# Words of eight marks instead of four in the scan of a sparse graph stack, built on TensorE and read by VectorE out of PSUM

## The chip, the cores and the metric

The kernel runs on one core of a Trainium2 chip. The metric is the device time of one execution in microseconds (us). The engines are called as the profile calls them: PE (matrix multiply; PEld loads its weights), DVE (vector), ACT (activation), POOL (which here mostly issues gathers, that is, DMAs whose rows are given by an index list), and SP (which issues the other DMAs). The program gives each engine its instructions in one fixed order.

## The reference

Four graph layers follow each other on x of 4096 rows by 128 features, with one adjacency matrix adj of 4096 x 4096 in f32, of which only few entries differ from zero (all of the diagonal does, and row 0 is the densest; the chance of an entry falls with both indices).

```python
h = relu(layernorm(x)); x = x + (h @ Ws.T + (adj @ h) @ Wn.T + b)                         # layer 0
h = relu(layernorm(x)); x = x + (h @ w0 + (adj @ h) @ w1 + (2 adj @ (adj @ h) - h) @ w2 + b)  # layer 1
h = relu(layernorm(x)); H = h @ W.T                                                        # layer 2
tau = adj.T * exp(leaky(alpha_src + alpha_dst));  x = x + (adj.T * tau / tau.sum(1)) @ H
h = relu(layernorm(x))                                                                     # layer 3
agg[i] = sum_j adj[i, j] * gelu(s[i] + d[j] + b);  x = x + layernorm(gelu([h, agg] @ U.T + b) + h) * w + b
```

Layer 3 takes each single non-zero entry (i, j) with its value. So the kernel has to find where the entries are.

## The kernel before, in words

All work is done for the entries that are likely to be there, and a dense version follows only if something was missed. The rows stand in an order fixed beforehand, in which each of the 32 blocks of 128 rows has about as many entries as fit whole chunks of 128.

**Scan.** `read_adj` (L761) loads each block's 128 x 4096 values in two halves of 1 MB on SP, into three buffers. `mark` (L770) turns a half into marks on ACT: one byte of fp8 an entry, 1.0 where the value is positive and 0.5 where it is zero. There are four mask tiles of 128 x 4096 bytes. `scan` (L781) takes a block's mask on DVE: it takes the mark off the diagonal (L787, after which `bare[b]` is set), and reads four marks at a time as one 32-bit word. L791 takes the largest word of each stripe of 256 columns into `col_raw`; L796 puts the word's own number (from the constant `spread`, 0 to 1023) into the bits that all marks share; L798 sets words without an entry to zero; and MAX8 (L805) takes the eight largest words of each segment of columns into `cand`. The segments were cut so that a row hardly ever has more than eight words with entries in one. After L798 and after the row flags the mask tile is given back (`mask_left`).

**Row and column lists.** A row stripe is 256 rows (two blocks), a column stripe 256 columns. `row_flags` (L693) finds with matmuls of the mask against a column of ones (L704) which blocks' columns have entries; `col_flags` (L713) takes the same for columns from `col_raw`, once `all_marked` is set, that is after L791 of the last block. Both then take one of three **lanes** (sets of small tiles, `lane = yield lanes`), set their flags (L709, L717), and run `pairs` (L635), a chain over DVE, PE, ACT and DVE that ends in lists of rows to fetch (`fetch_row`, `seg_row`; `fetch_col`, `seg_col`). The lane is then given back. `pairs` uses one of three `bank` and two `pick` banks of PSUM.

**Layers.** For layer 0 POOL gathers, for each chunk of a row stripe's list, 128 segments of adj.T (`rseg`) and 128 rows of h (`g`); the blocks next to the diagonal and the dense ones are loaded whole (`big`). PE sums both (L1146, L1163). `finish_0` adds the result, makes the next h and writes it to a table in memory, from which layer 1 gathers its rows once the whole table is there. The segments are kept in `r_tab` for layers 1 and 2. `fetch_columns` (L739) gathers column segments (`cseg`) for layer 2's attention.

**Entries.** `entries` (L813), for eleven groups of units (a unit is a row block, or a part of block 0), counts the marks of the candidate words on DVE, ranks them, spreads the words over partitions with matmuls into `pick` banks, one entry a place, and works out of each word the entry's column (L904 to L936). `values` (L938) then gathers the entries' values (`e_val`, 158 gathers). Later `Messages` gathers 158 times rows of d for layer 3.

**The order of the work** is written out when the program is built. `Plan` (L255) simulates the engines: each task is a generator that yields what it wants: an event, a slot of a pool (`Slots`), or an engine with an estimated duration. Among tasks that could begin at about the same time, the one with the lowest rank goes first; a slot goes to the task that is ready first. The program of each engine is the order that comes out. Ranks here: `row_flags` -9, `mark` -8.6, `scan` -4, `col_flags` -1.5 and up, the layers 0, `fetch_columns` 4, `values` 6. `on_dve(n)` is 0.16 + 1.05e-3 n us, and a PE duration is multiplied by 0.72. Where the plan sees a gap on PE, `fill` (L611) puts matmuls of zeros (L617, 128 x 512, f16) into 0.8 of it, into a free bank. The lines that set who gets a lane first:

```python
yield "PE", 3.2 + 0.4 * (i == 0)          # row_flags, then: lane = yield lanes
...
yield on_dve(WORDS)                       # scan, WORDS = 1024
nc.vector.tensor_reduce(col_raw[:, :, b], ...)
if b == NB - 1:
    all_marked.set(plan.finish)           # col_flags: yield all_marked; lane = yield lanes
```

Of the kernel before, what the change touches and what calls it, by code (L numbers as in the profile page):

```python
# [25 lines left out]
N = 4096  # L26
# [13 lines left out]
EMPTY = struct.unpack("<f", b"\x30" * 4)[0]  # L40
WORDS = N // 4
# [83 lines left out]
class Unit:  # L125
# [3 lines left out]
    def __init__(self, block, cuts):  # L129
        self.block, self.cuts = block, cuts  # L130
        self.segments = list(zip(cuts[:-1], cuts[1:]))
        self.places = _places(LIKELY[block * P:(block + 1) * P, 4 * cuts[0]:4 * cuts[-1]], 16)
        self.cap = -(-self.places // P)
# [6 lines left out]
def _cuts(block, limit):  # L140
    q = 1 - np.prod(1 - LIKELY[block * P:(block + 1) * P].reshape(P, WORDS, 4), axis=2)
# [17 lines left out]
    if WORDS - cuts[-2] < 8:  # L159
        cuts[-2] = WORDS - 8  # L160
# [9 lines left out]
def _groups():  # L170
    cuts = _cuts(0, 2e-5)
    hub = []
    while len(cuts) > 1:
        n = len(cuts) - 1
        while n > 1 and LIKELY[:P, 4 * cuts[0]:4 * cuts[n]].sum() > _fits(HUB) - 2:
            n -= 1
        hub.append(Unit(0, cuts[:n + 1]))
        cuts = cuts[n:]
# [200 lines left out]
def sparse_stack(tc, x, adj, adjT, adj_near, adjT_near, diag, w_self, w_neigh, b0, w1, b1, w2, att_src, att_dst,  # L379
# [10 lines left out]
    with ExitStack() as ctx:  # L390
# [65 lines left out]
        word = hT.bitcast(I32)[:, :WORDS]  # L456
        piece = hT.bitcast(I32)[:, WORDS:2 * WORDS]
        nc.gpsimd.iota(word, pattern=[[1, WORDS]], base=0, channel_multiplier=0)
# [7 lines left out]
        mod4 = kept("mod4", (P, 1))  # L466
        mod4_i = iota("mod4_i", (P, 1), [[0, 1]], step=1, dtype=I32)
# [31 lines left out]
        spread = kept("spread", (P, WORDS), I32)  # L499
        nc.vector.tensor_scalar(spread, word, 7, None, op0=ALU.bitwise_and)  # L500
        for bits, by in ((0x38, 5), (0x1c0, 10), (0x200, 15)):
            nc.vector.tensor_scalar(piece, word, bits, by, op0=ALU.bitwise_and, op1=ALU.logical_shift_left)
            nc.vector.tensor_tensor(spread, spread, piece, op=ALU.bitwise_or)
# [3 lines left out]
        nc.vector.tensor_scalar(mod4_i, mod4_i, 3, None, op0=ALU.bitwise_and)  # L507
        nc.vector.tensor_scalar(mod4, mod4_i, 4.0, None, op0=ALU.add)
# [30 lines left out]
        for cand in cands:  # L539
            nc.gpsimd.memset(cand, 0.0)  # L540
# [172 lines left out]
        def col_flags(s):  # L713
            yield all_marked
            lane = yield lanes
            yield on_dve(NB)
            nc.vector.tensor_scalar(lane["f"], col_raw[:, s.index, :], EMPTY, None, op0=ALU.is_gt)  # L717
            yield from pairs(s, lane, fetch_col, seg_col, CS, col_list[s.index])
# [5 lines left out]
        all_marked = Event()  # L724
# [56 lines left out]
        def scan():  # L781
            for b in range(NB):
# [7 lines left out]
                yield on_dve(WORDS)  # L790
                nc.vector.tensor_reduce(col_raw[:, :, b], mask.bitcast(F32).rearrange("p (s w) -> p s w", w=CS // 4),  # L791
                                        axis=AX.X, op=ALU.max)
                if b == NB - 1:
                    all_marked.set(plan.finish)
                yield on_dve(WORDS)
                nc.vector.tensor_tensor(words, mask.bitcast(I32), spread, op=ALU.bitwise_or)  # L796
                yield on_dve(WORDS + 250)
                nc.vector.scalar_tensor_tensor(words.bitcast(F32), mask.bitcast(F32), EMPTY, words.bitcast(F32),  # L798
                                               op0=ALU.is_gt, op1=ALU.mult)
                mask_left[b].set(plan.finish)  # L800
                for u in UNITS:
                    if u.block == b:
                        yield "DVE", 0.15 * len(u.segments) + (u.cuts[-1] - u.cuts[0]) / 960
                        for k, (lo, hi) in enumerate(u.segments):
                            nc.vector.max(cand_of[u.number][:, 8 * k:8 * k + 8], words.bitcast(F32)[:, lo:hi])  # L805
                        picked[u.number].set(plan.finish)
# [6 lines left out]
        def entries(number, group):  # L813
# [4 lines left out]
            for u in units:  # L818
                yield picked[u.number]
            lane = yield elanes  # L820
            cand_i = cand.bitcast(I32).rearrange("p g w -> p (g w)")
            t, v = (lane[k].bitcast(I32)[:, :G * W] for k in ("et", "ev"))
            pop, cum = (lane[k][:, :G * W].rearrange("p (g w) -> p g w", w=W) for k in ("epop", "ecum"))
            yield "DVE", 0.6 + 3.0e-3 * G * W
            nc.vector.tensor_scalar(t, cand_i, 3, 0x01010101, op0=ALU.logical_shift_right, op1=ALU.bitwise_and)
            nc.vector.tensor_reduce(pop.rearrange("p g w -> p (g w)"),
                                    t.bitcast(U8).rearrange("p (n k) -> p n k", k=4), axis=AX.X, op=ALU.add)
# [15 lines left out]
            yield "DVE", 0.8 + 3.6e-3 * G * W  # L843
            nc.vector.tensor_scalar(v, cand_i, 0x0f0f0f0f, None, op0=ALU.bitwise_and)
            nc.vector.scalar_tensor_tensor(v, v, 4, v, op0=ALU.logical_shift_right, op1=ALU.bitwise_or)
            nc.vector.tensor_scalar(t, v, 8, 0xff00, op0=ALU.logical_shift_right, op1=ALU.bitwise_and)
            nc.vector.scalar_tensor_tensor(v, v, 0xff, t, op0=ALU.bitwise_and, op1=ALU.bitwise_or)
# [13 lines left out]
            v3, t3 = (k.rearrange("p (g w) -> p g w", w=W) for k in (v, t))  # L861
# [4 lines left out]
            nc.vector.tensor_copy(t3, cum)  # L866
            nc.vector.tensor_scalar(t, t, 3, 13, op0=ALU.bitwise_and, op1=ALU.logical_shift_left)
            nc.vector.tensor_tensor(v, v, t, op=ALU.bitwise_or)
            yield "DVE", 1.1 + 5.0e-3 * G * W
            nc.vector.memset(vf[:, :, 0:1], 0.0)  # L870
            nc.vector.tensor_scalar(t, v, 0xff00, None, op0=ALU.bitwise_and)
            nc.vector.tensor_copy(vf[:, :, 1:], t3)
            nc.vector.tensor_sub(A[:, :, W:2 * W], vf[:, :, 1:], vf[:, :, :W])
            nc.vector.tensor_scalar(t, v, 0xff, None, op0=ALU.bitwise_and)
            nc.vector.tensor_copy(vf[:, :, 1:], t3)
# [30 lines left out]
            vi, a, b, r, at = (lane[k].bitcast(I32)[:, :n] for k in ("dv", "da", "db", "dr", "dat"))  # L906
            bit = [lane[f"dbit{k}"].bitcast(I32)[:, :n] for k in range(4)]
            yield "DVE", 1.9
            nc.vector.tensor_copy(vi, packed[:, es])
            for k in range(4):  # L910
                nc.vector.tensor_scalar(bit[k], vi, 4 * k + 3, 1, op0=ALU.logical_shift_right, op1=ALU.bitwise_and)
            for k in range(1, 4):
                nc.vector.tensor_add(bit[k], bit[k - 1], bit[k])
            nc.vector.tensor_scalar(e_valid[:, es], bit[3], 0.0, None, op0=ALU.is_gt)

            nc.vector.tensor_scalar(r, vi, 13, 3, op0=ALU.logical_shift_right, op1=ALU.bitwise_and)
            nc.vector.tensor_scalar(r, r, -1.0, mod4, op0=ALU.mult, op1=ALU.add)
            nc.vector.tensor_scalar(r, r, 3, None, op0=ALU.bitwise_and)
            yield "DVE", 1.2
            nc.vector.tensor_tensor(at, bit[0], r, op=ALU.is_le)  # L920
            for k in range(1, 3):
                nc.vector.tensor_tensor(a, bit[k], r, op=ALU.is_le)
# [1092 lines left out]
```

## Time and profile before

| | |
|---|---|
| median of 9 runs | 1173.34 us (1165.52 to 1175.98) |
| the profiled execution's own time | 1168.68 us |
| its span, first to last instruction | 1166.8 us |
| granted clock of PE, mean | 0.918 |
| busy: PE, DVE, POOL, ACT | 956.3, 888.2, 767.0, 578.5 us |
| busy in the first 320 us: PE, DVE, ACT, POOL | 254.8, 273.7, 201.1, 162.6 us |
| MAX8 (L805): 234 instructions | 51.0 us |
| first and last MAX8 | 36.0 and 325.2 us |
| first column segment gathered | 341.2 us |
| first gather of layer 1 | 385.3 us |
| last gather | 1138.6 us |

A slice of the page is 1166.8 / 40 = 29.2 us. In the tables of groups the columns are: line, engine, operation, output <- input, shape, count, then busy time and mean duration (ns), then the idle time of the engine just ahead of these and what ended it. In a timeline the columns are: start, duration (of several merged instructions the whole), engine, line, operation, and in brackets idle time before it with what it waited for. "issue" is time in which the engine waited for nothing that the profile shows.

### The profile page before, as it was taken

What the parts mean: (1) busy time and instruction counts of PE and PEld (TensorE: products, weight loads), DVE (VectorE), ACT (ScalarE), POOL (GpSimd) and SP (SyncE); (2) the same over time, 40 slices, a digit from 0 to 9 for tenths busy, and PEclk for the clock granted to TensorE, in tenths of its full rate; (3) what the DMA queues carried; (4) which work ended last, traced back from release to release, by engine and by line L of the source; (5) the groups of instructions that cost most, each with busy time, mean ns of one, the idle gap of its engine ahead of it and who ended that gap; (6) DMA issues with size and microseconds to landing.
All of it is one profiled execution on the core that took longest, in us unless ns stands there. A gap on an engine that the chain in (4) does not pass through costs nothing.

```text
span 1166.8 us, 19272 instructions
## 1 busy us (share of the span) xinstructions
PE 956.3 (82%) x5782; PEld 666.3 (57%) x5782; DVE 888.2 (76%) x3443; ACT 578.5 (50%) x1228; POOL 767.0 (66%) x831
## 2 busy tenths in 40 slices
PE   5888887777988988888888879989999876778883
PEld 2455665554645766666666654445545555566662
DVE  6899988989878787676898866666657585577895
ACT  4985565666423122231434447577676652244553
POOL 5127755535536777777777777777777777777770
PEclk9989889889888899898999989999999877889998
DMA  7999999999747878888875643444455222222231
GB/s 225 386 355 386 357 402 358 335 334 346 277 131 201 259 240 264 253 278 295 245 218 174 180 144 103 116 129 119 118 144 150 56 75 62 53 69 68 78 79 28
DMA packets 122169, 236.04 MB, mean 202 GB/s; under 512 B 22452, under 2 KB 75592, under 8 KB 113864
## 3 DMA queue, kind: packets, MB, share of 16 engines
q1 hardware_dynamic: 95656, 186.45, 46.4%
q0 software_dynamic: 26400, 48.27, 16.6%
q8 instruction: 48, 0.79, 0.3%
q14 instruction: 65, 0.53, 0.1%
HBM read 203.41 MB, written 31.23 MB: 201 GB/s over the span
## 4 chain that ended last, share of the span: by engine, by line
PE 15%; DVE 12%; DMA 8%; POOL 5%; ACT 5%; issue 5%; DVEq 0%; POOLq 0%; ACTq 0%
PE acc L1262 4%; PE acc L1260 4%; DMA m<-d_tab,e_col 3%; POOL e_val L551 3%; DMA tau<-d_tab,e_col 2%; PE bank L604 1%; DMA e_val<-in_adj,e_at 1%; ACT e L1236 1%; DMA g<-a_tab,fetch_col 1%; POOL g L551 1%; POOL m L551 1%; ACT e L1239 1%; PE acc L1429 1%; DVE r L1410 1%; PE bank L617 1%
## 5 line engine op out<-in xcount | busy, mean ns | idle before, releaser
L551 POOL DMA_INDIRECT e_val<-in_adj,e_at x158 | 160.8, 1018 | 48.0 <-issue 40.1
L551 POOL DMA_INDIRECT g<-h_tab,fetch_row x136 | 132.6, 975 | 41.1 <-issue 25.8
L551 POOL DMA_INDIRECT rseg<-in_adjT,seg_row x68 | 69.0, 1015 | 88.4 <-issue 37.4
L1146 PE MATMUL acc<-big,hA 128*128 128x256 f32 x448 | 120.0, 410 | 4.9 <-DMA big<-in_adjT_near 4.9
L617 PEld LDWEIGHTS <-nothing 128*128 128x128 f16 x732 | 73.6, 103 | 78.7 <-issue 15.1
L617 PE MATMUL pick<-nothing 128*128 128x512 f16 x430 | 109.7, 401 | 0.0
L551 POOL DMA_INDIRECT cseg<-in_adj,seg_col x74 | 70.5, 953 | 46.7 <-issue 18.4
L1146 PEld LDWEIGHTS acc<-big,hA 128*128 128x128 f32 x448 | 87.6, 206 | 16.9 <-DMA big<-in_adjT_near 5.7
L776 ACT ACTIVATE mask<-dst 128x2048 fp8e4<-128x2048 f32 x43 | 81.9, 1904 | 22.9 <-DMA dst<-in_adj 22.7
L551 POOL DMA_INDIRECT m<-d_tab,e_col x79 | 77.0, 975 | 24.1 <-issue 13.1
L551 POOL DMA_INDIRECT g<-a_tab,fetch_col x74 | 76.4, 1032 | 22.6 <-issue 12.8
L1243 DVE TENSOR_TENSOR tau<-e,big 128x512 f32<-128x512 f32 (+3 forms) x61 | 54.4, 891 | 43.0 <-ACT e L1239 38.9
L551 POOL DMA_INDIRECT tau<-d_tab,e_col x67 | 64.9, 968 | 22.4 <-issue 10.4
L551 POOL DMA_INDIRECT g<-u_tab,fetch_row x68 | 64.9, 954 | 20.7 <-issue 10.7
L617 PE MATMUL bank<-nothing 128*128 128x512 f16 x302 | 77.8, 393 | 0.0
L1163 PE MATMUL acc<-big,g 128*128 128x256 f32 x272 | 73.0, 399 | 4.9 <-DMA g<-u_tab,fetch_row 1.8
L577 ACT ACTIVATE junk<-xN,stat 128x128 f32<-128x128 f32 x128 | 51.3, 401 | 46.8 <-DVE stat L573 40.0
L1146 PE MATMUL acc<-big,hB 128*128 128x256 f32 x224 | 64.8, 431 | 11.5 <-DMA big<-in_adjT_near 11.5
L895 ACT COPY ehit<-pick 128x192 f32<-128x192 f32 (+7 forms) x74 | 20.5, 287 | 90.7 <-PE pick L892 78.8
L898 DVE SCALAR_TENSOR_TENSOR ehit<-ehit,pos,pick 128x32 f32<-128x32 f32 (+7 forms) x158 | 38.8, 285 | 31.4 <-ACT ehit L895 31.0
L1163 PE MATMUL acc<-rseg,g 128*128 128x256 f32 x136 | 50.0, 474 | 15.0 <-DMA g<-h_tab,fetch_row 15.0
L1163 PEld LDWEIGHTS acc<-big,g 128*128 128x128 f32 x272 | 50.6, 197 | 14.9 <-issue 3.8
(322 smaller groups left out, 2560.1 us busy)
## 6 DMA issues: line engine op xcount, KB each, us to landing
dst<-in_adj SPq DMA_DIRECT2D x43, 1024.0 KB
big<-in_adjT_near SPq DMA_DIRECT2D x45, 512.0 KB
raw<-in_adj SPq DMA_DIRECT2D x21, 1024.0 KB
big<-in_adjT_near SPq DMA_DIRECT2D x66, 256.0 KB
big<-r_tab SPq DMA_DIRECT2D x30, 512.0 KB
c_tab<-cseg SPq DMA_DIRECT2D x74, 128.0 KB
r_tab<-rseg SPq DMA_DIRECT2D x68, 128.0 KB
big<-c_tab SPq DMA_DIRECT2D x15, 512.0 KB
```

What stands on the lines that cost most here:

```text
L551: nc.gpsimd.indirect_dma_start(out=dst, out_offset=None, in_=table[:, :], in_offset=bass.IndirectOffsetOnAxis(ap=index, axis=0))
L577: nc.scalar.activation(junk, src[:, k, :], AF.Square, bias=st[:, 0, k:k + 1], accum_out=st[:, 1, k:k + 1])
L604: nc.tensor.matmul(p[:, k * D:(k + 1) * D], lhs[:, k * P:(k + 1) * P], w, start=i == 0, stop=i == len(terms) - 1)
L617: nc.tensor.matmul(idle[2][idle[1]], nothing[:, :P], nothing, start=True, stop=True)
L776: nc.scalar.activation(mask[:, h * HALF:(h + 1) * HALF], raw_of[b, h], AF.Sigmoid, scale=1e38, accum_out=marks[:, 2 * b + h:2 * b + h + 1] ...
L895: nc.scalar.copy(hit, pv[:, :, :W])
L898: nc.vector.scalar_tensor_tensor(hit[:, q, :], hit[:, q, :], pos0[:, k + q:k + q + 1], pv[:, q, W:2 * W], op0=ALU.is_le, op1=ALU.mult, acc ...
L1146: nc.tensor.matmul(acc, self.near[:, b, :D], as_rows(t)[:, k, :], start=count == 0, stop=count == every - 1)
L1163: nc.tensor.matmul(acc, row[:, :D], r, start=count == 0, stop=count == every - 1)
L1243: nc.vector.tensor_mul(tau[:, :n, :], e[:, :n, :], a[:, :n, :])
L1260: nc.tensor.matmul(acc[0:1, CS:2 * CS], parts[k][:, D + 1:], tau[:, k, :], start=False, stop=False)
L1262: nc.tensor.matmul(acc[:, :CS], parts[k][:, :D], e[:, k, :], start=False, stop=self.count[s.index] == every - 1)
```

## The change

A word now holds eight marks, so a block has 512 words, which fill one bank of PSUM. PE makes them: for k = 0 to 7, a diagonal matrix with 2 to the k on the diagonal (`planes`, fp8) is multiplied with every eighth mark of the mask, from the k-th on, and all eight products are summed in a `pick` bank; a ninth matmul adds the word's number times a small step (`places`). So a word without entries is 127.5 plus its place, and one with entries is larger by half the sum of their powers of two. DVE reads the words from PSUM: one maximum for `col_raw`, and MAX8. The passes L796 and L798 and the constant `spread` go. The work is a task of its own, `extract`, which `scan` starts for each block. `all_marked` is set when all 32 blocks have been reduced. The counting in `entries` and the decoding of the column are written anew for words of this kind.

```diff
-EMPTY = struct.unpack("<f", b"\x30" * 4)[0]
-WORDS = N // 4
+PER = 8
+WORDS = N // PER
+BLANK = 0.5 * (2 ** PER - 1)
+STEP = 0.5 / WORDS
...
-        spread = kept("spread", (P, WORDS), I32)
-        nc.vector.tensor_scalar(spread, word, 7, None, op0=ALU.bitwise_and)
-        for bits, by in ((0x38, 5), (0x1c0, 10), (0x200, 15)):
-            nc.vector.tensor_scalar(piece, word, bits, by, op0=ALU.bitwise_and, op1=ALU.logical_shift_left)
-            nc.vector.tensor_tensor(spread, spread, piece, op=ALU.bitwise_or)
+        planes = kept("planes", (P, PER, P), F8)
+        for k in range(PER):
+            nc.vector.tensor_scalar(planes[:, k, :], ident, float(2 ** k), None, op0=ALU.mult, saturate=False)
+        places = kept("places", (1, WORDS), F16)
+        nc.vector.tensor_scalar(places, iota_row[0:1, :WORDS], STEP, None, op0=ALU.mult)
+        ones16 = kept("ones16", (1, P), F16)
+        nc.vector.memset(ones16, 1.0)
+        powers = kept("powers", (P, PER), I32)
+        for k in range(PER):
+            nc.vector.memset(powers[:, k:k + 1], 2 ** k)
...
-            nc.vector.tensor_scalar(lane["f"], col_raw[:, s.index, :], EMPTY, None, op0=ALU.is_gt)
+            nc.vector.tensor_scalar(lane["f"], col_raw[:, s.index, :], BLANK + 0.5 - 0.5 * STEP, None, op0=ALU.is_gt)
...
-        all_marked = Event()
+        all_marked = Count(NB)
...
                 plan.start(give_back(mask_left[b], masks, mask), 0)
-                yield on_dve(WORDS)
-                nc.vector.tensor_reduce(col_raw[:, :, b], mask.bitcast(F32).rearrange("p (s w) -> p s w", w=CS // 4),
-                                        axis=AX.X, op=ALU.max)
-                if b == NB - 1:
-                    all_marked.set(plan.finish)
-                yield on_dve(WORDS)
-                nc.vector.tensor_tensor(words, mask.bitcast(I32), spread, op=ALU.bitwise_or)
-                yield on_dve(WORDS + 250)
-                nc.vector.scalar_tensor_tensor(words.bitcast(F32), mask.bitcast(F32), EMPTY, words.bitcast(F32),
-                                               op0=ALU.is_gt, op1=ALU.mult)
-                mask_left[b].set(plan.finish)
-                for u in UNITS:
...
+                plan.start(extract(b, mask), -4 + b * 1e-3)
+
+        def extract(b, mask):
+
+            words = yield picks
+            yield "PE", (PER + 1) * 0.32
+            planes_of = mask.rearrange("p (w k) -> p w k", k=PER)
+            for k in range(PER):
+                nc.tensor.matmul(words, planes[:, k, :], planes_of[:, :, k], start=k == 0, stop=False)
+            nc.tensor.matmul(words, ones16, places, start=False, stop=True)
+            mask_left[b].set(plan.finish)
+            yield on_dve(WORDS)
+            nc.vector.tensor_reduce(col_raw[:, :, b], words.rearrange("p (s w) -> p s w", w=CS // PER),
+                                    axis=AX.X, op=ALU.max)
+            all_marked.set(plan.finish)
+            for u in UNITS:
+                if u.block == b:
+                    yield "DVE", 0.15 * len(u.segments) + (u.cuts[-1] - u.cuts[0]) / 960
+                    for k, (lo, hi) in enumerate(u.segments):
+                        nc.vector.max(cand_of[u.number][:, 8 * k:8 * k + 8], words[:, lo:hi])
+                    picked[u.number].set(plan.finish)
+            plan.release(picks, words)
...
-            yield "DVE", 0.6 + 3.0e-3 * G * W
-            nc.vector.tensor_scalar(t, cand_i, 3, 0x01010101, op0=ALU.logical_shift_right, op1=ALU.bitwise_and)
-            nc.vector.tensor_reduce(pop.rearrange("p g w -> p (g w)"),
-                                    t.bitcast(U8).rearrange("p (n k) -> p n k", k=4), axis=AX.X, op=ALU.add)
+            yield "DVE", 1.0 + 1.0e-3 * 10 * G * W
+            nc.vector.tensor_scalar(t, cand.rearrange("p g w -> p (g w)"), -BLANK, 1.0 / STEP, op0=ALU.add,
+                                    op1=ALU.mult)
+            nc.vector.tensor_scalar(v, t, 9, 0xff, op0=ALU.logical_shift_right, op1=ALU.bitwise_and)
+            nc.vector.tensor_scalar(x, t, 10, 0x55, op0=ALU.logical_shift_right, op1=ALU.bitwise_and)
+            nc.vector.tensor_sub(v, v, x)
...
+            nc.vector.tensor_add(pop.rearrange("p g w -> p (g w)"), v, x)
```

In the parts left out, the sizes follow the words of eight (the cuts of the segments, the groups of block 0's units, `mod4` becomes `turn`), four DVE steps over the candidate words that packed the words into 16 bits are dropped from `entries`, and the column of an entry is worked out with a running sum (`tensor_tensor_scan`) over eight flags an entry where four single bits were handled one by one: 17 DVE steps a group in place of about 27.

## The prediction

> **What bounds the kernel now.** I read four views in this order: the forty slices of the page, the windows of 10 us around the end of the scan, the orders of POOL, DVE and PE in time there, and the groups by line. The slices show two stages.
>
> ```profile
> DVE  6899988989878787676898866666657585577895
> POOL 5127755535536777777777777777777777777770
> DMA  7999999999747878888875643444455222222231
> ```
>
> Up to the eleventh slice (320 us) DMA is at nine tenths, from 20 to 310 us at 0.99 of the sixteen engines in the windows view, and DVE is nearly as full. From the thirteenth slice on POOL stands at seven tenths to the end. That is not slack: POOL starts one gather every 1.25 us (0.95 us busy, 0.30 us "issue"), so seven tenths is a full queue. The windows view counts 608 gathers from 341 to 1140 us; the first starts at 341.16, the last at 1138.6, so 608 x 1.25 = 760 of 797 us are gathers, and 37 us are lost in all. So the end is the moment when POOL becomes full, plus about 797, plus the 27 us after the last gather. That moment is 341 us, and between the two stages lies a hole:
>
> ```profile
> 320.77 0.94 POOL L551 DMA_INDIRECT g<-h_tab,fetch_row  x1 [0.30 <-issue]
> 325.16 1.26 POOL L1008 TENSOR_TENSOR xN<-xN,b_sb 128x512 f32<-128x512 f32 x1 [3.46 <-issue]
> 341.16 0.96 POOL L551 DMA_INDIRECT cseg<-in_adj,seg_col  x1 [14.73 <-DVE pf L641]
> ...
> 348.67 0.95 POOL L551 DMA_INDIRECT rseg<-in_adjT,seg_row  x1 [0.30 <-issue]
> ```
>
> POOL idles 341.16 - 321.71 - 1.26 = 18.2 us, then takes six column segments (cseg), and only at 348.67 the eight gathers (four rseg, four g) of the last row stripe, number 15. Layer 0 ends with that stripe, and the first gather of layer 1 is at 385.3. Why so late, when the last half block was marked at 314.5? PE and DVE say it:
>
> ```profile
> 318.18 0.94 PE L704 MATMUL bank<-ones,mask 128*128 128x1 fp8e4 x32
> ```
>
> ```profile
> 318.52 1.22 DVE L791 TENSOR_REDUCE col_raw<-mask 128x16 f32<-128x1024 f32 x1
> 319.66 1.21 DVE L796 TENSOR_TENSOR words<-mask,spread 128x1024 int32<-128x1024 int32 x1
> ...
> 323.26 1.22 DVE L798 SCALAR_TENSOR_TENSOR words<-mask,words 128x1024 f32<-128x1024 f32 x1
> 324.51 1.35 DVE L805 MAX8 cand<-words 128x8 f32<-128x129 f32 x3
> 325.78 0.69 DVE L717 TENSOR_SCALAR pf<-col_raw 128x32 f32<-128x32 f32 x1
> ...
> 340.80 0.18 DVE L709 TENSOR_SCALAR pf<-bank 128x32 f32<-128x32 f32 x1
> ```
>
> PE has the row flags of stripe 15 at 319.1, but DVE reads them (L709) at 340.8. A row list needs one of three lanes. The planner sets all_marked when the last block's reduce (L791) ends, one DVE pass of 1.24 us by its cost after the diagonal is off, while row_flags needs a matmul group of 3.2 x 0.72 = 2.3 us by its cost. So three column stripes take the three lanes first (three L717 from 325.78 to 327.24), and stripe 15 gets one only when column stripe 0 is done.
>
> **The change, part by part.** Duration rows first.
>
> ```profile
> L796 DVE TENSOR_TENSOR words<-mask,spread 128x1024 int32<-128x1024 int32 x32 | 39.5, 1233 | 0.0
> L791 DVE TENSOR_REDUCE col_raw<-mask 128x16 f32<-128x1024 f32 x32 | 39.1, 1221 | 2.2 <-ACT mask L776 0.4
> L798 DVE SCALAR_TENSOR_TENSOR words<-mask,words 128x1024 f32<-128x1024 f32 x32 | 39.1, 1221 | 0.9
> L617 PE MATMUL pick<-nothing 128*128 128x512 f16 x430 | 109.7, 401 | 0.0
> ```
>
> *DVE in the scan.* Removed: the three passes, 117.7 us. Added: one reduce over 512 words, at 0.69 us (L572 takes 0.684 for 512 elements from SBUF; L1000, which reads a bank, 0.682), 22 us. MAX8 costs 51.0 us now; its rows go from 0.15 us for 8 elements to 0.71 for 549, some 1.04 ns an element, so half the 32 x 1024 elements is -17 us and 16 segments fewer (234 to 218, by my working of the cuts) at 0.08 us is -1. Setup: spread costs 1.0 + 3 x (0.74 + 1.22) = 6.9 us; planes and powers cost 8 x 0.31 (L1388, same shape) + 8 x 0.06 (L641) = 3.0. Sum: about -117 us of the 273.7 us that DVE is busy up to 320 us. For operands in PSUM I see no surcharge: L667 reads a pick bank in 0.284 us, L669 the same shape from SBUF in 0.292; bounds 0 and, doubling the smallest MAX8 pitch of 0.08 us, +0.08 x 250 = 20 us. Either end leaves DVE far from full.
>
> [...]
>
> *What that is worth up to 310 us: nothing, in my forecast.* The saved time lies beside DMA at 0.99. The scan's 64 MB and layer 0's loads stay as they are, and no DMA is added or moved. Bounds: 0, and 290 x (1.03 - 0.99)/1.03 = 11 us if DMA went to the best share that the windows show (1.03).
>
> *PE in the scan.* Added: nine matmuls of 128x512 a block. The filler has that shape: 104.4 us for 407 in the first 320 us, 0.257 us each at the granted clock of 0.91, so 2.3 us a block and 74 us in all. No row has a moving operand that takes every eighth byte. Lower end 0.257 us: 512 columns as in the filler. Upper end: the f32 matmuls (eight L1146 of 256 columns in 1.89 us) take 0.92 ns a column of 4 bytes; if the bytes passed over set the pace, 8 bytes a column are 1.84 ns and 0.94 us a matmul, 7.8 us a block. I take 0.257, because f16 is the nearest row: one column, one short element. PE is busy 254.8 of the first 320 us, of which 104.4 is filler; the planner fills 0.8 of a gap, and 32 x 9 x 0.32 x 0.72 = 66 us of gap go, so some 53 us of filler go too: 254.8 + 74 - 53 = 276 of 320. It fits.
>
> [...]
>
> *New waits.* The reduce waits for PE; behind it on DVE stand row lists and norms, whose readers are POOL and ACT. PE waits up to 2.2 us in the scan for a gathered row (L1163). 32 such waits are 71 us, inside the 163 us that DVE then has free. The mask is given back when PE has read it instead of after L798; four masks cover a late one. A pick bank is held from before the matmuls to the last MAX8, beside the row lists' selections; two banks at some 9 us a block cover that.
>
> *The turn at 320 us, on the path.* all_marked now comes from extract: behind row_flags on PE (rank -9 before -4), nine matmuls, then the reduce. By the planner's costs that is 2.3 + 2.1 + 0.7 + hops = 5.5 us after the diagonal, and row_flags asks for its lane at 2.5. So **stripe 15 gets its lane first**. Diagonal off at 318.3, flags at 319.1, L709 at 319.3. Stripe 14 ran from L709 at 302.38 to its list at 311.26 and its first gather at 312.03, 9.65 us with scan work between; so gathers from 329.0 and, eight by 1.25, to 339.0. The column lists: words at 319.1 + 2.3 = 321.4, reduce to 322.1, MAX8 0.5, the norm between (2.6 us) to 325.2 at worst; from 325.78 the first list took 15.1 us, so 337.8 to 340.3. POOL goes straight on at about 339. Its full stretch starts at 329.0 instead of 341.16: **-12.2 us**. Layer 0 ends earlier by more, so layers 1 and 2, which keep PE at 250 of 300 us from 400 to 700, and the attention, 205 of 220, start earlier as well and can't hold the gain back.
>
> *entries and decode.* Per group five DVE steps of some 0.25 us and one reduce over bytes (0.8 to 1.45 us) go, ten of 0.25 come; decode loses some 27 steps of 0.18 us and gains 17 of 0.17 to 0.4. Between -1 and +1.5 us for each of eleven groups, hidden under POOL's queue (236 gathers in 300 us, 400 to 700); without that cover up to 16 us. Chunks (158), their gathers and units stay; 68 instead of 74 pick groups are filled, at some 1.3 us of PE, ACT and DVE each, under the same cover. POOL's iota of 1024 words (1.0 us at 1.5 us) goes, ahead of loads that end later.
>
> Sum: 1168.7 (the profiled execution; span 1166.8) - 12.2 = 1156.5. The median of the nine runs, 1173.34, is 4.7 above the profiled one, so I predict 1173.3 - 12.2 = **1161**.
>
> **Rivals.** (1) *The scan shortens too.* For it: DVE stands at 9.3 to 9.7 of 10 us in many windows. Against: DMA at 0.99. -12 - 11: 1150. (2) *The hole closes and the time is lost again*: cseg waits for later column lists (POOL lost 3.8 us at 376 to a late list), or stripe 15 stays late. Only the 2 to 4 us by which the first column list is earlier remain: 1170. (3) *PE becomes the bound of the scan*, slower. Place: the eight strided matmuls. From 320 - 150 - 51 = 118 us, or 3.7 us a block, **0.41 us a matmul**, PE is full. At 0.55 it is 5.0 us a block, 150 + 51 + 160 - 320 = +41 us of scan, 1202; at the upper end 7.8 us, +131 us. A little above 0.41 the in-order waits on PE already eat the 12 us: from 1177. (4) *Not done as said*: if words cost DVE what they cost before, the time stays at 1173.
>
> **How the numbers follow.** Forecast (1161, give or take 7) 0.47; rival 1 0.15; rival 2 0.16, half of it faster; rival 3 0.18; rival 4 0.04. A measurement can tell 0.3%, 3.5 us. Faster: 0.47 + 0.15 + 0.08 = 0.70; same: 0.08 + 0.04 = 0.12; slower 0.18. The range reaches to rival 1's 1150 and, for the mild end of rival 3, to 1178.
>
> **What would show it.** Right: a reduce of 128x512 at some 0.69 us; strided matmuls one every 0.22 to 0.26 us; DVE near five tenths in the scan, DMA still at nine; L709's successor for stripe 15 ahead of the first column lists; rseg gathers near 329 and no hole of 15 us on POOL. Wrong: strided matmuls over 0.41 us, ACT's marks waiting for masks, or a new hole on POOL after 340.

## The result and the profile after

| | before | after |
|---|---|---|
| median | 1172.89 us (31 runs, 1161.29 to 1180.07) | 1209.96 us (10 runs, 1198.31 to 1213.83) |
| span of the profiled execution | 1166.8 us | 1201.8 us |
| POOL instructions that began by 900 us | 646 | 638 |
| last gather starts | 1138.6 us | 1173.8 us |

The change made the kernel slower: ratio 1.0312, interval [1.0281, 1.0344]. I had forecast 1161 with a range up to 1178.

The slices of the page of after, for the three engines shown of before and for PE (a slice is 1201.8 / 40 = 30.0 us):

```profile
PE   4999999999988869878887888899999886677874
DVE  4445444435577867567786887367666376468895
POOL 5125754345356777777777777777777726777770
DMA  8899997999858878898875533343455213222231
```

In the first eleven slices DVE has come down to four tenths (forecast: near five), but PE is at nine tenths. And POOL, which before stood at seven tenths without a break from the fourteenth slice on, has a two in the 33rd (961 to 991 us). These are two losses at two places.

**The first loss, in the scan.** The group of the strided matmuls in the first 320 us of after (busy us, mean ns), and the longest of the waits up to 335 us (us in total, times, longest):

```profile
L801 PE MATMUL pick<-mask,planes 128*128 128x512 fp8e4 x238 | 112.1, 627 | 0.0
```

```profile
DVE col_raw L805 <- PE pick L802: 87.8, 27, 7.7
```

238 of them take 112.1 us, 0.471 us each, where I had taken 0.257 (the mean duration of one, 627 ns, is longer, as each overlaps the next: 238 x 0.627 = 149 us of durations in 112.1 us). VectorE waits for the words 27 times. The windows of the first 320 us, before and then after (busy PE, PEld, DVE, ACT, POOL; granted clock, DMA share, GB/s):

```profile
0.00:320.00 320.00, 254.83 (x2011) 168.87 (x2012) 273.69 (x864) 201.05 (x345) 162.57 (x216) 0.91 0.94 342
```

```profile
0.00:320.00 320.00, 301.50 (x1960) 160.62 (x1961) 149.65 (x763) 191.12 (x330) 145.15 (x208) 0.95 0.93 331
```

DVE lost 124 us (117 forecast), PE gained 47 net although filler fell from 104.4 to 52.4 us, and DMA moved less, not more. PE is the bound of the scan now. PE and then DVE in time at its end:

```profile
327.98 3.77 PE L801 MATMUL pick<-mask,planes 128*128 128x512 fp8e4 x8
331.69 0.39 PE L802 MATMUL pick<-places,ones 1*128 1x512 f16 x1
...
335.04 0.94 PE L707 MATMUL bank<-ones,mask 128*128 128x1 fp8e4 x32
335.84 3.77 PE L801 MATMUL pick<-mask,planes 128*128 128x512 fp8e4 x8
```

```profile
336.88 0.18 DVE L712 TENSOR_SCALAR pf<-bank 128x32 f32<-128x32 f32 x1
...
345.00 0.17 DVE L720 TENSOR_SCALAR pf<-col_raw 128x32 f32<-128x32 f32 x1
```

Eight matmuls take 3.77 us. The last half block was marked at 335.2 instead of 314.6. Stripe 15 does get its lane first (L712 ahead of L720), as forecast. But all of it comes 20 us late, and POOL waits for its list:

```profile
336.31 0.94 POOL L554 DMA_INDIRECT g<-h_tab,fetch_row  x1 [0.30 <-issue]
343.53 1.26 POOL L1023 TENSOR_TENSOR xN<-xN,b_sb 128x512 f32<-128x512 f32 x1 [6.27 <-ACT hB L588]
348.40 0.96 POOL L554 DMA_INDIRECT rseg<-in_adjT,seg_row  x1 [3.61 <-DVE mids L628]
```

POOL is full from 348.4 on, not from the forecast 329.0 (before: 341.2). By 900 us it is 8 instructions behind before, 8 x 1.25 = 10 us.

**The second loss, at the end of the attention.** The same order of POOL later on:

```profile
962.53 0.94 POOL L554 DMA_INDIRECT m<-d_tab,e_col  x1 [0.30 <-issue]
985.18 1.03 POOL L554 DMA_INDIRECT m<-d_tab,e_col  x1 [21.71 <-PE bank L1430]
```

Layer 3's gathers wait for the end of layer 2. Three views of after tell why that is late: PE (L1430 is a message's product into a bank; L607 the product for the d table; L1299 is `finish_3`), ACT (L1294 copies a finished stripe's sum into one of two `agg` tiles; L1327 copies the d product into one), and DVE (L1436 adds the gathered rows to the message's bank, which is then given back).

```profile
830.03 1.16 PE L1430 MATMUL bank<-s,msel 128*128 128x128 f32 x8
...
843.06 0.83 PE L1430 MATMUL bank<-s,msel 128*128 128x128 f32 x6
...
911.65 1.05 PE L607 MATMUL bank<-msg_d_sb,hT 128*128 128x128 f32 x8
...
937.44 10.96 PE L620 MATMUL pick<-nothing 128*128 128x512 f16 x50
953.53 0.80 PE L1299 MATMUL bank<-ident,agg 128*128 128x128 f32 x2 [5.14 <-DVE m L1436]
```

```profile
906.21 0.56 ACT L1294 COPY agg<-acc 128x512 f32<-128x512 f32 x1
...
912.46 0.56 ACT L1294 COPY agg<-acc 128x512 f32<-128x512 f32 x1
956.12 0.59 ACT L1327 COPY agg<-bank 128x512 f32<-128x512 f32 x1 [1.44 <-PE bank L1300]
```

```profile
952.79 0.69 DVE L1436 TENSOR_TENSOR m<-m,bank 128x512 f32<-128x512 f32 x1 [4.76 <-DMA m<-d_tab,e_col]
```

Two of the three banks went at 830 and 843 to two early messages of block 0, whose rows are gathered only after all other gathers, from 946.3 on. That was so before as well (823.7 and 838.0, released from 951.6). There the third bank was enough, even for two stripes that copied their sums at 877.3 and 880.8. In after two stripes copied theirs at 906.2 and 912.5, and between them, at 911.7, the third bank took the d product. So both agg tiles were full and waited for a bank, and the bank waited for an agg tile. Each had what the other needed. From 913.0 until the message's add at 952.8 no stripe was finished, PE ran out of other work at 937.4 (zeros, then a wait), and three batches of attention stood behind the wait (their products run from 963.0 to 973.4).

### The profile page after: what moved, and what is told of

Read it like the earlier page. It is cut to its first block, busy times and chain, and to the rows that moved or that the text cites. A ratio compares the mean times of both kernels' runs of the same rounds, so it can differ in the third digit from the quotient of the medians.

```text
span 1201.8 us, 19383 instructions
## 1 busy us (share of the span) xinstructions
PE 1028.9 (86%) x5926; PEld 670.4 (56%) x5926; DVE 759.0 (63%) x3300; ACT 577.0 (48%) x1222; POOL 762.1 (63%) x830
## 4 chain that ended last, share of the span: by engine, by line
PE 43%; DMA 20%; DVE 14%; POOL 10%; issue 7%; ACT 6%; SPq 0%; DVEq 0%; POOLq 0%; ACTq 0%
PE pick L801 8%; PE acc L1161 6%; POOL e_val L554 5%; PE acc L1178 4%; PE bank L620 4%; PE bank L607 3%; PE acc L1275 3%; DMA cseg<-in_adj,seg_col 3%; PE acc L1277 3%; DMA g<-a_tab,fetch_col 3%; DMA tau<-d_tab,e_col 2%; POOL g L554 2%; DMA big<-in_adjT_near 2%; PE bank L707 2%; DMA m<-d_tab,e_col 2%
## 5 line engine op out<-in xcount | busy, mean ns | idle before, releaser
L554 POOL DMA_INDIRECT rseg<-in_adjT,seg_row x68 | 64.4, 948 | 93.4 <-issue 43.2
L801 PE MATMUL pick<-mask,planes 128*128 128x512 fp8e4 x256 | 120.6, 627 | 0.0
L620 PE MATMUL bank<-nothing 128*128 128x512 f16 x427 | 109.6, 400 | 0.0
L620 PEld LDWEIGHTS <-nothing 128*128 128x128 f16 x588 | 59.4, 102 | 64.2 <-issue 10.4
L1161 PEld LDWEIGHTS acc<-big,hA 128*128 128x128 f32 x448 | 82.8, 196 | 17.0 <-DMA big<-in_adjT_near 4.5
L554 POOL DMA_INDIRECT m<-d_tab,e_col x63 | 60.4, 958 | 40.6 <-PE bank L1430 22.3
L805 DVE TENSOR_REDUCE col_raw<-pick 128x16 f32<-128x512 f32 x32 | 22.1, 691 | 87.9 <-PE pick L802 87.8
L554 POOL DMA_INDIRECT tau<-d_tab,e_col x59 | 59.2, 1003 | 18.0 <-issue 11.6
L801 PEld LDWEIGHTS <-planes 128*128 128x128 fp8e4 x256 | 26.6, 112 | 64.9 <-issue 64.6
L1251 ACT ACTIVATE e<-dst,g 128x256 f32<-128x256 f32 x74 | 36.6, 503 | 51.2 <-DMA g<-a_tab,fetch_col 50.7
```

Of the source, the lines that this page charges most:

```text
L554: nc.gpsimd.indirect_dma_start(out=dst, out_offset=None, in_=table[:, :], in_offset=bass.IndirectOffsetOnAxis(ap=index, axis=0))
L620: nc.tensor.matmul(idle[2][idle[1]], nothing[:, :P], nothing, start=True, stop=True)
L801: nc.tensor.matmul(words, planes[:, k, :], planes_of[:, :, k], start=k == 0, stop=False)
L1161: nc.tensor.matmul(acc, self.near[:, b, :D], as_rows(t)[:, k, :], start=count == 0, stop=count == every - 1)
L1251: nc.scalar.activation(e[:, k, :], dst[:, s.lo:s.lo + CS], AF.Relu, bias=h[:, D:D + 1])
```

## The experiments

Each run was compared with the kernel before on its own chip. For most that took 1171.7 to 1172.9 us. For nine runs it took 1485 to 1510 us, at a lower granted clock (0.81 to 0.83 instead of 0.90 to 0.93) and with more time in which engines waited for nothing that the profile shows. They were made on three chips, one of which had given 1172.8 us a few minutes before. I read no absolute time from these runs; they are told at the end.

**e_strides.** A kernel of its own: 48 matmuls of 128x512 for each step between the moving operand's elements, and VectorE's maxima from SBUF and from PSUM. It computes nothing of the reference.

> Computes nothing of the reference (the output is zeros): 48 matmuls of 128 x 512 in a row for each of several strides of the moving operand (fp8: every 1st, 2nd, 4th, 8th, 16th byte, and runs of 16 bytes 128 apart; f16 and f32: every 1st, 2nd, 4th, 8th element), then MAX8 of 8, 64 and 256 words and the reduce of 512 words, from SBUF and from PSUM. Theory A (the stride itself makes a matmul of the changed kernel start every 0.46 us): fp8 by 8 takes 0.43 to 0.47 us a matmul at full clock, by 1 and in runs of 16 some 0.22. Rival (the stride costs nothing, the matmuls were slow because the other engines used the same memory at that time): fp8 by 8 takes 0.22 us here. [...]

Windows of PE (length, busy with count, granted clock, DMA): steps 1, 2, 4, 8 and 16 bytes, then runs of 16 bytes.

```profile
20.00:28.00 8.00, 8.00 (x39) 1.00 0.01 2
30.00:38.00 8.00, 8.00 (x39) 1.00 0.00 0
41.00:49.00 8.00, 8.00 (x37) 1.00 0.00 0
51.00:71.00 20.00, 20.00 (x46) 1.00 0.00 1
75.00:110.00 35.00, 35.00 (x40) 0.50 0.00 0
115.00:127.00 12.00, 12.00 (x46) 0.81 0.00 1
```

8 / 39 to 8 / 37 = 0.205 to 0.216 us up to a step of four bytes, 20 / 46 = 0.435 us at eight, at the same clock: twice. At 16 it is 35 / 40 = 0.875 us, but at half the clock, so the step's share of that is open. Runs of 16 bytes cost 12 / 46 = 0.261 us at a clock of 0.81; if the time goes with the clock, by my estimate, that is 0.261 x 0.81 = 0.21 us, the pace of step 1. From the groups of VectorE in the page (copied lies in SBUF, words in PSUM):

```profile
L60 DVE MAX8 best<-words 128x8 f32<-128x8 f32 (+2 forms) x96 | 17.2, 264 | 0.0
L60 DVE MAX8 best<-copied 128x8 f32<-128x8 f32 (+2 forms) x96 | 16.8, 260 | 0.0
L62 DVE TENSOR_REDUCE best<-words 128x16 f32<-128x512 f32 x16 | 9.6, 683 | 0.0
L62 DVE TENSOR_REDUCE best<-copied 128x16 f32<-128x512 f32 x16 | 9.6, 681 | 0.0
```

By these means reading PSUM costs 2 and 4 ns more (7 ns for the smallest MAX8, of 8 words: 159 against 152), so the prediction, which saw no surcharge for operands in PSUM, holds to within these few ns.

**e_contig_read.** The marks as eight runs of 16 in each 128 columns, so that the matmuls read runs; ScalarE reads every eighth word for it.

```diff
-nc.tensor.matmul(words, planes[:, k, :], planes_of[:, :, k], ...)
+nc.tensor.matmul(words, planes[:, k, :], planes_of[:, :, k, :], ...)   # "p (b k w) -> p b k w"
```

> The changed kernel, with the same order of work on every engine, but ACT writes the marks of each 128 columns sorted into eight runs of 16, so that each matmul reads runs of 16 bytes instead of every eighth byte; ACT reads its input with a stride of eight words instead. Theory A (the strided matmuls fill PE and so lengthen the scan by 21 us, the mark of the last half ends at 335 instead of 314): matmuls of 0.22 to 0.26 us, last mark at 310 to 320 us, POOL full from about 330 us. For the second loss (POOL waits 27 us for PE at 963 to 998 us, when the attention ends) there are two theories. A1, it follows from the late scan: it goes too, 1161 us. A2, it is in the new order of the work: it stays, 1161 + 27 = 1188 us. Rival B (PE isn't what holds the scan; it is the wait of VectorE for the words, or the pick banks): the scan still ends at 330 or later, over 1200 us. If ACT's strided read takes much longer than 1.9 us a half block, ACT becomes the bound (64 halves) and this tells nothing of PE.

Measured 1221.54 us, ratio 1.0416 [1.0394, 1.0437]. The bound went to ScalarE (its marks in the first 320 us):

```profile
L786 ACT ACTIVATE mask<-dst 128x2048 fp8e4<-128x2048 f32 x38 | 147.7, 3886 | 1.6 <-DMA dst<-in_adj 1.4
```

3.89 us a half instead of 1.90. PE was down to 254.9 us, as in before, and 223 strided matmuls took 65.0 us, 0.29 us each, so the matmuls' reads were cured; the cure cost more.

**e_nofill.** After, without zeros in the gaps of the scan.

```diff
-            plan.filler = fill          # ahead of the scan
+        plan.filler = fill              # behind it
```

> The changed kernel without the matmuls of zeros (filler) during the scan, with them afterwards. Theory A (PE full in the scan): 55 us of PE work go, so the last mark comes at 314 to 322 us instead of 335, time 1188 to 1197 us if the second loss stays, 1161 to 1170 us if it goes with the first. The granted clock may fall without filler; if it falls to 0.8, the gain is about used up. Rival B (the scan is held by waits and not by the amount of PE work): last mark still at 330 to 335, time 1205 to 1210 us.

Measured 1194.51 us, ratio 1.0196 [1.0169, 1.0223]. The last mark ended at 325.8 us, about half of the way back from 335.2 to 314.6, and POOL stood at 647 by 900 us, level with before: as a sum the first loss is gone. The granted clock up to 320 us was 0.90 (0.95 in after). The hole stayed (POOL busy 5.1 of 20 us from 960 to 980). So the second loss doesn't follow from POOL's lag; e_runs4 below shows it with an early scan.

**e_lane.** Before, with `col_flags` waiting until the last row stripe has its lane: the turn of the prediction by itself.

```diff
+            yield last_row          # col_flags, after all_marked
```

> The kernel before, with one edit in the plan: no column stripe asks for a lane before the last row stripe has its own. This is the prediction's step at the turn, alone. Theory of the prediction: the last rseg gathers come some 15 to 20 us earlier (329 to 335 instead of 349 to 356 us), POOL is full from about 330 us, and the end comes 10 to 12 us earlier: 1161 us. Rival C: POOL's start moves, but layers 1 and 2 or the attention hold the end: 1170 to 1175 us.

Measured 1182.91 us, ratio 1.0091 [1.0054, 1.0128]. By 900 us POOL stood at 647 against 646: one gather gained, not twelve microseconds. But in this execution the scan ended late, and the edit can't be the reason, since it acts only behind the last mark. The last half's mark and the first gather of POOL's full stretch, here and then in e_before_bank_late (below), whose edit acts only from 823.7 us on:

```profile
321.71 1.91 ACT L780 ACTIVATE mask<-dst 128x2048 fp8e4<-128x2048 f32 x1
339.50 0.96 POOL L551 DMA_INDIRECT rseg<-in_adjT,seg_row  x1 [5.36 <-DVE mids L625]
```

```profile
318.87 1.91 ACT L776 ACTIVATE mask<-dst 128x2048 fp8e4<-128x2048 f32 x1
341.50 0.96 POOL L551 DMA_INDIRECT cseg<-in_adj,seg_col  x1 [10.39 <-DVE pf L641]
```

So the same instructions ended the scan (with the short instruction that reads the mark's sum) at 314.6 us in before, at 320.9 in e_before_bank_late and at 323.7 here: single executions differ by 9 us. From there to POOL's full stretch it took 26.5 and 20.6 us with the old turn, 15.8 with the new one.

A hole at the attention's end appeared here too, without TensorE's words: POOL waited 13.2 us for the d table and was busy 5.4 of 20 us from 960 to 980. It isn't quite the wait of after. Here the stripes' copies are 9 to 17 us apart, and ScalarE, whose order is fixed, waited for an early message's rows with a stripe's copy (L1283) behind it:

```profile
956.76 0.52 ACT L1428 ACTIVATE m<-m 128x384 f32<-128x384 f32 x1 [10.35 <-DVE m L1425]
957.19 0.57 ACT L1283 COPY agg<-acc 128x512 f32<-128x512 f32 x1
```

**e_bank_late and e_before_bank_late.** One order changed in `message`, in after and in before.

```diff
-                p = yield banks
+                for q in range(n):
+                    yield here[q]
+                p = yield banks
...
-                for q in range(n):
-                    yield here[q]
```

> The kernel after, with one order changed: a message first waits for its gathered rows and then takes a bank of PSUM, where it took the bank first and held it while its gather was under way. Theory (the second loss is a wait for banks): in the trace of after PE does nothing but fillers from 937.4 to 948.4 and then waits until 953.5 for a bank that a hub message holds until its rows have landed, while four batches of attention stand queued behind that wait. These 16 us go: the last attention product ends about 957 instead of 973, the hole of 21.7 us on POOL shrinks to some 5, time 1190 to 1197. Rival (the second loss is the late scan, handed on): nothing changes by more than 3 us, 1207 to 1213.

> The kernel before with the same order (a message takes its bank only when its rows have landed). Theory: here PE met that wait only after the attention's last product (4.3 us, ending at 952.4), so at most these 4 us come: 1167 to 1173. Rival (the old order costs every kernel as much): 1155 to 1160.

Measured 1182.94 us for after with it, ratio to before 1.0087 [1.0044, 1.0131]: 27.0 us less than after. For before with it 1172.11, ratio 0.999 [0.9958, 1.0021]: nothing. POOL from 940 to 980 us, after and then with late banks:

```profile
940.00:960.00 20.00, 15.15 (x16) 0.83 0.19 47
960.00:980.00 20.00, 2.83 (x3) 0.91 0.07 14
```

```profile
940.00:960.00 20.00, 15.13 (x17) 1.00 0.20 56
960.00:980.00 20.00, 14.82 (x16) 1.00 0.35 90
```

The hole is gone. The gain is more than the 16 us that I had read off PE's stop alone: POOL's idle time is what counts, 21.7 us and a second wait of 4.4 us at 998.2, and both are gone. (POOL was also four instructions further by 900 us, 642, but that is not the edit's: it acts from 830 us on, and this execution's scan had ended at 331.1. PE had three batches behind the wait, not the four that the expectation counts.)

**e_runs4 and e_runs4_bank_late.** After, with marks in runs of four, so that a matmul reads every fourth byte, and ScalarE marks a half with two instructions; and the same with late banks.

```diff
-nc.scalar.activation(mask[:, h * HALF:(h + 1) * HALF], raw_of[b, h], ...)
+for i in range(2):        # mask "p (b i v) -> p i b v", raw "p (w i j) -> p i w j", runs of 4
+    nc.scalar.activation(mask_of4[:, i], raw_of4[:, i], ...)
...
-nc.tensor.matmul(words, planes[:, k, :], planes_of[:, :, k], ...)
+nc.tensor.matmul(words, planes[:, k, :], planes_of[:, :, :, k // 4, k % 4], ...)
```

> The kernel after, with the marks laid out in runs of four within each 128 columns, so that a plane's matmul reads every fourth byte instead of every eighth; ScalarE writes each half in two instructions for it (16 bytes read of each 32). Theory: by the strides measured alone (0.219 us at four, 0.451 at eight) the nine matmuls of a block go from 4.1 to 2.0 us, PE has 30 us and more free of the first 320, and the last mark ends at 314 to 318 instead of 335: the first loss of 20.7 us goes and the second of some 27 stays, 1188 to 1198. If two ScalarE instructions of a half take over 3.9 us together, ScalarE bounds the scan instead, as it did with reads of every eighth word: 1215 and more. Rival (the second loss follows from the first): 1165 to 1178.

> Both edits together: marks in runs of four, and a message that takes its bank only when its rows have landed. Theory: both losses go, 1165 to 1180; whether it is below the kernel before depends on the turn, which brought nothing when it was tried alone (1182.9), so 1172 is the likeliest. Rival (the losses are one): the same as the runs of four alone, within 4 us.

Measured 1172.76 us, ratio 1.0015 [0.9974, 1.0055], and with late banks 1147.47, ratio **0.9764 [0.9722, 0.9806]**. The matmuls of the first 320 us:

```profile
L813 PE MATMUL pick<-mask,planes 128*128 128x512 fp8e4 x256 | 68.8, 413 | 0.0
```

All 256 are done, at 0.27 us each. The time of runs of four alone lies in the rival's range (1165 to 1178), but not for the rival's reason: the second loss was still there, a wait of 21.7 us on POOL that ended at 950.6. What neither theory had is that the scan didn't come back to before's length but became shorter. With late banks, too, the time is below both theories. The last mark ended at 302.7 and 306.3 us (314.6 to 323.7 in the three executions of the old scan), and from 20 to 300 us DMA carried 374 and 372 GB/s (before 364). Runs of four with late banks is faster than both kernels.

| medians, us | bank first | bank late |
|---|---|---|
| before | 1172.9 | 1172.1 |
| after, every eighth byte | 1210.0 | 1182.9 |
| after, every fourth byte | 1172.8 | 1147.5 |

The two edits add up: 37.2 and 27.0 alone, 62.5 together.

**g_less_dve.** Is it VectorE's saved time that shortens the scan? Before, with late banks, and without L798.

```diff
-nc.vector.scalar_tensor_tensor(words.bitcast(F32), mask.bitcast(F32), EMPTY, words.bitcast(F32), ...)
...
-            nc.vector.tensor_copy(n_bad, p[:, :1])
+            nc.vector.tensor_scalar(n_bad, p[:, :1], 0.0, None, op0=ALU.mult)
```

> The kernel before, its messages taking their bank late (1172.1 with that edit alone), without the pass that sets words without marks to zero (32 x 1.22 us of VectorE in the scan), and with the number of overflows that picks the slow path set to zero; it picks other words than the reference does, the number of gathers is the same. Theory of the prediction (DMA sets the end of the scan, VectorE lies beside it): the last mark ends at 314 to 321 as before, some 261 POOL instructions by 400 us, 1168 to 1175. Rival (VectorE holds the scan, and DMA carries more when VectorE is let off): the last mark at 303 to 308, 270 or more POOL instructions by 400 us, 9 to 15 gathers earlier at 1.27 us each: 1153 to 1161.

Measured 1153.37 us, ratio 0.9825 [0.978, 0.987]. From 20 to 300 us, before with late banks and then this (columns as above):

```profile
20.00:300.00 280.00, 231.81 (x1771) 154.99 (x1768) 238.34 (x784) 181.37 (x314) 132.01 (x122) 0.87 0.97 355
```

```profile
20.00:300.00 280.00, 239.74 (x1935) 155.28 (x1934) 218.71 (x806) 193.83 (x326) 140.48 (x130) 0.90 1.00 377
```

DMA carried 377 GB/s instead of 355 (before itself: 364 at a share of 0.99), more than the share tells, which rose from 0.97 to 1.00. The last mark ends at 300.5 us (before 314.6, before with late banks 320.9). So VectorE held the scan, though it was busy only 238 of 280 us, and 39 us less of it are worth 18.7 us of the kernel. The way goes over ScalarE's order: its waits for VectorE's `mids` (L625) in these 280 us fell from 21.8 to 7.8 us, and the loads' waits for its marks from 60.0 to 51.2. The edit also gives a mask back one pass earlier, but in none of these traces does a mark wait for a mask tile.

**The runs for which before took 1485 to 1510 us.** e_less_dve, without the line on n_bad, ran the dense version behind it (21957 us); f_less_dve, which has it and is the same program as g_less_dve, gave 1.0007 [0.9955, 1.0059]. VectorE waited 86 us for nothing that the profile shows in f_less_dve, 6 us in g_less_dve. The turn with late banks (e_lane_bank_late, f_lane_bank_late, g_lane_bank_late) gave 1.015 [0.9977, 1.0324], 1.0211 [1.0111, 1.031] and 1.0132 [0.9964, 1.03]. After without zeros and with late banks (e_nofill_bank_late, f_nofill_bank_late) gave 1.0333 [1.0213, 1.0453] and 1.0293 [1.0161, 1.0424]. All three had been expected near or below 1172:

> The kernel before, with the column stripes waiting until the last row stripe has its lane, and messages that take their bank late. Theory (the turn's new order alone is worth little; the 10 us that it lost were the wait for banks): 263 POOL instructions by 400 us against 261, so 2 x 1.27 us of gain and the hole of 13 us gone, 1166 to 1172. Rival (the turn is worth the 12 us of the prediction, and the banks took them away): 1157 to 1162.

> The kernel after, without filler matmuls in the scan and with messages that take their bank late. Theory (two separate losses): 262 POOL instructions by 400 us as in the kernel before, and no hole: 1194.5 less 25, so 1166 to 1173. Rival (the hole is an effect of the order that this plan makes elsewhere): above 1185.

None came true there. What slows these runs is open, so they decide nothing about the others. The plan with the measured price of a matmul (e_cost, f_cost) is another matter:

```diff
-            yield "PE", (PER + 1) * 0.32
+            yield "PE", (PER + 1) * 0.64
```

> The kernel after, with the planner told what a plane's matmul took (0.46 us instead of 0.23), nothing else changed. TensorE still bounds the scan in both theories, so the last mark ends at 331 to 338. Theory (the hole comes of banks held during gathers, whatever price the plan has for the scan): 1203 to 1213. Rival (the hole comes of a plan made with a wrong price): 1180 to 1190.

It gave 1.0675 [1.0552, 1.0799] and 1.069 [1.0576, 1.0803], and a reason shows in the order of the work (waits of f_cost up to 400 us):

```profile
POOL rseg L554 <- PE pick L667: 161.7, 2, 161.4
```

With PE full in its own reckoning, the plan put the row lists' matmuls behind the scan, and POOL stood still for 161 us. The marks ended at 249.2 us, not at the 331 to 338 of both theories, so the run says nothing on either.

## Why the prediction was wrong, point by point

**The end is POOL's queue.** Right, and it accounts for every run at the usual times. Taking before's span, 1166.8 us, and 1.25 us for each POOL instruction more or fewer by 900 us, what is left over is the hole:

| | by 900 us | span by that | span | left over |
|---|---|---|---|---|
| after | 638 | 1176.8 | 1201.8 | 25.0 |
| e_contig_read | 622 | 1196.8 | 1221.1 | 24.3 |
| e_nofill | 647 | 1165.6 | 1189.8 | 24.2 |
| e_lane | 647 | 1165.6 | 1181.1 | 15.5 |
| e_runs4 | 663 | 1145.6 | 1166.5 | 20.9 |
| e_bank_late | 642 | 1171.8 | 1174.8 | 3.0 |
| e_before_bank_late | 644 | 1169.3 | 1170.5 | 1.2 |
| g_less_dve | 659 | 1150.6 | 1152.1 | 1.5 |
| e_runs4_bank_late | 662 | 1146.8 | 1145.3 | -1.5 |

**The nine matmuls at 0.257 us** is the first step that failed: 0.46 to 0.47 measured. Both ends were in the text, 0.257 and 0.94; the choice of the f16 filler as the nearest row was the error, since no row had the step. The threshold of 0.41 us isn't contradicted: at 0.47 PE was full, at 0.27 it wasn't; no run lies nearer. Without the hole the loss is 11.3 us (1182.94 against 1171.67), in line with rival 3's "from 1177". Alone, in e_strides, a step of eight bytes took 0.435 us and a step of four 0.216, both at a clock of 1.00.

**"Worth nothing beside DMA at 0.99"** failed too, the other way. A DMA share of 0.99 left room: with VectorE let off, 1.00 carried 377 GB/s instead of 364, and the marks ended 14 us earlier (20 against before with late banks). My bound for it, 11 us, was too small; I had given it 0.15. Rival 1 was right in its mechanism. With both losses out its two terms, turn and scan, come together: 1147.5 measured, 1150 given. That it fits so closely is partly luck, since the scan's end differs by 9 us from one execution to the next.

**The turn, -12.2 us.** The order came as forecast, and nearly the step too: from the last mark to stripe 15's first gather it took 13.2 us in after, e_bank_late and e_runs4_bank_late and 15.8 in e_lane, where the prediction has 14.5 (329.0 - 314.5). With the old turn POOL's full stretch began 26.5 us after the last mark in before, 20.6 in e_before_bank_late and 23.1 in g_less_dve. So the turn is worth 5 to 13 us by these traces, and before's, from which I took the 12.2, has the largest distance of the three. What it brought was eaten by a late scan, in after by the matmuls (stripe 15's gathers began at 348.4, not 329.0), in e_lane's execution by chance. No usual run has the turn alone with late banks. In the fastest version it does what was meant: stripe 15's gathers start at 319.5, and the column segments follow at 329.6 without a gap.

**"The attention starts earlier as well and can't hold the gain back"** is the second step that failed, and the dearest (25 us). I judged the attention by PE's busy time, 205 of 220 us, and not by who holds the banks. Rival 2 had named a hole that closes and time that is lost again, but at the column lists.

**VectorE's times** were right: the reduce takes 0.691 us in after, and the 218 MAX8 34.0 us instead of 51.0. The counting and decoding stayed under POOL's queue (385 instructions from 400 to 900 us, before 386). Reading PSUM cost 2 to 7 ns an instruction more than SBUF in e_strides, where the forecast's bounds were 0 and 80.

Open: why the plan's order puts the d product between two stripes' copies in after, e_contig_read, e_nofill and e_runs4 (0.8 to 2.5 us ahead of the second) and not in before. It is one order out of many near-equal ones; what the runs show is that it stops mattering once messages don't hold banks over their gathers, in after and in the runs of four. Whether that also cures e_lane's hole, where ScalarE's order has a part, isn't shown.

## What to carry to other kernels

Price a matmul by the step of its moving operand (0.216 us at four bytes, 0.435 at eight in e_strides), and measure a step that the trace doesn't show before relying on the nearest row. When work moves to another engine, ask of the old one whether it was the bound beside a transfer that only looked full: compare bytes per second as well as the busy share (here 364 GB/s at 0.99 became 377 at 1.00). And when an order of work is written by a plan, list which tasks take two scarce tiles in turn; a tile that is held across a transfer can stop a whole stage in one order and cost nothing in another (27.0 us in after, nothing in before).

## What the runs showed of the hardware

- A matmul of 512 columns whose moving fp8 operand has a step of eight bytes took 0.435 us, 0.205 to 0.216 at steps of one to four, at a granted clock of 1.00 (e_strides).
- ScalarE took 3.89 us for 2048 elements a partition read at every eighth f32 word (e_contig_read), 1.90 us in order (before); with four words of every eight, 1024 elements took 1.05 us (e_runs4), as much as an activation over 1024 in order elsewhere in the kernel (L1239 of before, 1.06).
- The DMA engines' busy share of 0.97, 0.99 and 1.00 stood beside 355, 364 and 377 GB/s from 20 to 300 us in three executions (e_before_bank_late, before, g_less_dve).
